# A four-layer graph network on one core: one operand of VectorE's long two-operand instructions moved to PSUM

## The chip, the cores and the metric

The kernel runs on one core of a Trainium2 chip. The metric is the device time in microseconds of one execution, as the median of several runs. The profile is of one further execution; it names the engines PE (TensorE matmul), PEld (TensorE weight load), DVE (VectorE), ACT (ScalarE), POOL (GpSimd) and SP (SyncE). [...] SBUF is the main memory on the core.

## The reference

There are 6250 nodes with 128 features and 100000 directed edges (`src`, `dst`). Four graph layers are added to `x` one after the other, each fed with the rectified layer norm of `x`:

```python
edge_index = jnp.stack([src, dst])
h = relu(_layernorm(x)); x = x + L0(h, src, dst, ...)          # attention, 8 heads
h = relu(_layernorm(x)); x = x + L1(h, edge_index, ...)        # degree-weighted sum, batch norm, relu
h = relu(_layernorm(x)); x = x + L2(h, src, dst, ...)          # attention twice (one head), relu between
h = relu(_layernorm(x)); x = x + L3(h, edge_attr_32, edge_attr_4, edge_weight, edge_weight_n2, src, dst, ...)
```

Layers 0 and 2 weigh the rows of a node's neighbours by a softmax over its incoming edges:

```python
e = leaky_relu(scores_u[src] + scores_v[dst])
m = segment_max(e, dst)
ex = exp(e - m[dst])
out = segment_sum(h[src] * (ex / segment_sum(ex, dst)[dst]), dst)
```

Layer 1 sums scaled rows, `segment_sum(xw[src] * norm[:, None], dst)`, and normalizes over all nodes. Layer 3 works on pairs, the edges once more, with a small perceptron's output `w` for every edge:

```python
w = silu(rbf_ij @ rad_W1 + rad_b1) @ rad_W2 + rad_b2 + (silu(d_gamma @ sph_W1 + sph_b1) @ sph_W2 + sph_b2)
alpha = (q[idx_i] * w * k[idx_j]).sum(-1) / sqrt(32) * cutoff  # 4 heads of 32
agg = segment_sum(alpha[:, :, None] * v[idx_j], idx_i)         # here summed at src, read at dst
```

All arithmetic is float32 in the reference.

## The kernel before

**Blocks.** The nodes are sorted by their number of incoming edges and dealt to 49 blocks of 128 (`NR`). Block `b` has `CAPS[b]` slots for edges: 44, 25, 24, 23 and so on down, 820 in all (`TC`). One slot of a block is one gather: an indirect DMA that POOL issues (`fetch`, line 1577) and that brings 128 rows, one for each node, from a table in HBM. POOL issues some 4360 gathers, one after the other.

**Stages.** After a survey of the edges (0 to 385 us) and the placing of nodes (to 453 us), the stages follow POOL's gathers: layer 0 (`block0`, 453 to 2042 us), layer 1 (`part1`, to 3448), layer 2's first attention, here 2a (`block2` with name `g2`, to 4795), its second, 2b (`block2` with name `g3`, to 6107), and layer 3 (`fast_pairs`, 6125 to 7507).

**One block.** `block0` gathers rows with their scores, DVE forms the scores less their maximum, ACT takes the exponential (1600), DVE multiplies all rows with it (1603, up to 5632 elements per partition), sums them (1605) and the exponentials (1606); then two products on PE, each through `times_in_hops`: transpose into a PSUM tile `th_p` (1079), copy (1082), product into another `th_p` (1086). `block2` is alike, with one head: exponential 1750, product 1753, sums 1755 and 1756. In 2b a block ends with a product of 384 columns: query, key and value of layer 3. The query goes to `own` (1774), key and value are copied to `pr_kv` (1775), and `pair_rows` gathers the block's perceptron outputs from HBM (`pr_e`, 1792, one POOL instruction), multiplies them with the key (1797), and stores product and value as rows of a table in HBM (1801 and 1802, on SP's queue).

**Layer 3.** `fast_pairs` takes these rows by source node, 18 tiles of 128 for each of 49 blocks, three tiles at a time (a group). Gather `fp_rows` (1818, 14 buffers); compare lane numbers with an iota for a one-hot matrix (1823); transpose it (1828), copy it (1831), multiply with the queries (1835); DVE multiplies rows and queries (1838, which reads the PSUM tile `fp_qe`), sums over each head (1840), scales (1841), multiplies the values by these factors (1843); PE adds them up over the one-hot matrix (1849).

**Work behind the blocks.** `Pace` deals three streams of work into the turns of the blocks: the perceptron (`edge_weights`, 1221 to 1278, in layers 0, 1 and 2a), in layer 0 `source_ranks` (1336 to 1353), in layer 1 `source_places`, from about 2080 to 2750 us, and from 4250 us on `source_rows` (1429 to 1449). `source_places` finds the place of each edge among those of its source block: for each of the 49 blocks a row that is 1 where the edge's block equals `n` (1395, bf16 in SBUF), a running sum over it (1397), and a copy of the sum where the row is 1 (1398). A first loop of the same length (1375) makes the same row in order to count it.

**Order.** The order on PE, DVE and ACT is the order of emission (`manual_schedule`): `in_turns` starts block after block and advances the ones in progress by one step in turn, with the work behind dealt in between. A block's rows have three buffers (`rows_tile`), so POOL may run ahead of DVE by two blocks.

Of the kernel before, what the change touches and what calls it, by code (L numbers as in the profile page):

```python
# [27 lines left out]
N, D, E = 6250, 128, 100000  # L28
# [8 lines left out]
NH, HD = 8, 16  # L37
H3, D3 = 4, 32
# [786 lines left out]
NR = 49  # L825
# [11 lines left out]
TC = COL[NR]  # L837
TB = 18
# [233 lines left out]

def times_in_hops(k, p, ps, h, w, width, got):

    nc = k.nc
    nb = h.shape[1]
    t = ps.tile([128, 512], F32, name="th_p").rearrange("p (b d) -> p b d", b=4)
    for b in range(nb):
        nc.tensor.transpose(t[:, b, :], h[:, b, :], k.ident)
    yield  # L1080
    hT = p.tile([128, nb, 128], F32, name="th_T", bufs=3)
    nc.scalar.copy(hT, t[:, :nb, :])
    yield
    y = ps.tile([128, 512], F32, name="th_p")
    for b in range(nb):
        nc.tensor.matmul(y[:, b * width:(b + 1) * width], lhsT=hT[:, b, :], rhs=w, start=True, stop=True)
    got.append(y[:, 0:nb * width].rearrange("p (b f) -> p b f", f=width))
    yield
# [268 lines left out]

def source_places(k, c, q, y):


    nc, tc = k.nc, k.tc
# [3 lines left out]
    b = q.tile([128, TC], I32, name="sp_b")  # L1365
# [24 lines left out]
    pos = k.tile3  # L1390
    nc.vector.memset(pos, -1.0)
    yield
    for n in range(NR):
        eq = q.tile([128, TC], BF16, name="sp_eq", bufs=2)
        nc.vector.tensor_scalar(eq, d, float(n), None, op0=ALU.is_equal)
# [69 lines left out]
def finish(line):  # L1465
    while step(line):
        pass
# [47 lines left out]
def fast_layers(k, x, src, edges, l0, l1, l2a, l2b, l3):  # L1515
# [4 lines left out]
    with ExitStack() as ctx:  # L1520
# [60 lines left out]
        with tc.tile_pool(name="g0s", bufs=1) as q, tc.tile_pool(name="g0s_ps", bufs=2, space=PSUM) as qs, \  # L1581
                tc.tile_pool(name="g0", bufs=2) as p, tc.tile_pool(name="g0_ps", bufs=2, space=PSUM) as ps:
            bigs = big.enter_context(tc.tile_pool(name="g0b", bufs=1, side="right"))

            def block0(b):
# [13 lines left out]
                yield  # L1599
                nc.scalar.activation(e, e, AF.Exp)  # L1600
                yield
# [39 lines left out]
        with tc.tile_pool(name="g1s", bufs=1) as q, tc.tile_pool(name="g1s_ps", bufs=1, space=PSUM) as qs, \  # L1641
                tc.tile_pool(name="g1", bufs=2) as p:
            both = qs.tile([128, 512], F32, name="g1_both")
            total = both[:, 0:2 * D].rearrange("p (a d) -> p a d", a=2)
            spots = source_places(k, later, q, both[:, 2 * D:2 * D + 2 * NR].rearrange("p (a d) -> p a d", a=2))
            parts = [(b, c0, min(WE, CAPS[b] - c0)) for b in range(NR) for c0 in range(0, CAPS[b], WE)]
# [40 lines left out]
            in_turns([part1(*a) for a in parts], turns1, behind)  # L1687
            finish(spots)
            for n in range(2):
                nc.tensor.matmul(total[:, n, :], lhsT=k.ones, rhs=sums[:, n, :], start=True, stop=True)  # L1690
# [43 lines left out]
        for name, table, bias in (("g2", t2, b2), ("g3", t3, b3)):  # L1734
            with tc.tile_pool(name=name, bufs=2) as p, tc.tile_pool(name=name + "_big", bufs=1) as bigs, \
                    tc.tile_pool(name=name + "_ps", bufs=3, space=PSUM) as ps:

                def block2(b, name, table, bias, p, bigs, ps):
                    n = CAPS[b] + 1
# [38 lines left out]
                in_turns([block2(b, name, table, bias, p, bigs, ps) for b in range(NR)], turns_of, behind2)  # L1778
        finish(back.ids)


def pair_rows(k, p, kv, b):

    nc = k.nc
    for c0 in range(0, CAPS[b], WE):
        m = min(WE, CAPS[b] - c0)
        at = k.start_i[:, b:b + 1]
        if c0:
            at = p.tile([128, 1], I32, name="pr_at", bufs=1)
            nc.vector.tensor_scalar(at, k.start_i[:, b:b + 1], c0, None, op0=ALU.add)  # L1790
        e = p.tile([128, WE, D + 2], F32, name="pr_e")
        nc.gpsimd.indirect_dma_start(
            out=e[:, 0:m, :].rearrange("p w d -> p (w d)"), out_offset=None, in_=k.edges,
            in_offset=bass.IndirectOffsetOnAxis(ap=at, axis=0))
        yield
        nc.scalar.copy(e[:, 0:m, D + 1], k.lane[:, COL[b] + c0:COL[b] + c0 + m])
        nc.vector.tensor_tensor(e[:, 0:m, 0:D], e[:, 0:m, 0:D], kv[:, 0:1, :].to_broadcast([128, m, D]), op=ALU.mult)
# [4 lines left out]
        nc.sync.dma_start(to[:, :, D + 2:2 * D + 2], kv[:, 1:2, :].to_broadcast([128, m, D]))  # L1802


def fast_pairs(k, out):
# [3 lines left out]
    TG = 3  # L1809
    with tc.manual_schedule(engines={ET.PE, ET.DVE, ET.Activation}), \  # L1810
            tc.tile_pool(name="fp", bufs=3) as p, tc.tile_pool(name="fp_ps", bufs=2, space=PSUM) as ps:
        held = {}

        def tiles(h, t0):
            rows = p.tile([128, TG, 2 * D + 2], F32, name="fp_rows", bufs=14)
            for t in range(TG):
# [5 lines left out]
            oh = p.tile([128, TG, 128], F32, name="fp_oh", bufs=7)  # L1822
            nc.vector.tensor_tensor(oh, k.iota_l[:, None, :].to_broadcast([128, TG, 128]),
                                    rows[:, :, D + 1:D + 2].to_broadcast([128, TG, 128]), op=ALU.is_equal)
# [13 lines left out]
            nc.vector.tensor_tensor(pr, rows[:, :, 0:D], qe, op=ALU.mult)  # L1838
            al = p.tile([128, TG, H3], F32, name="fp_al")
            nc.vector.tensor_reduce(al, pr.rearrange("p t (h d) -> p t h d", h=H3), axis=AX.X, op=ALU.add)  # L1840
# [117 lines left out]
```

## Time and profile before

| what | us |
|---|---|
| median of 3 runs (7494.39 to 7505.08) | 7500.06 |
| the profiled execution, its own time | 7512.74 |
| its span, first to last instruction | 7510.9 |
| POOL busy | 4424.7 |
| DVE busy | 4015.5 |
| PE busy / PEld busy | 2838.1 / 1890.9 |
| ACT busy | 1178.3 |
| mean granted TensorE clock | 0.648 |

No engine is busy all the time: POOL has 59% of the span, DVE 53%. The span in 40 slices of 188 us shows that the shares change from stage to stage (each digit is a busy share in tenths):

```profile
PE   2301333333423434443344334332323115555555
DVE  9616656565423852233333577656778534545555
POOL 0075555445565775554465676657777756666665
DMA  0232232222221222223122222267878863333333
```

POOL's row is highest in slices 25 to 31, which is 2a's end and 2b; there the DMA row is high too. In a line of a group, the number after `x` is the count of instructions; then come busy us, the mean of one in ns, and the idle time of the engine just before them with what ended most of it. "issue" is time in which the engine waited for nothing that the profile shows, and "remote" is a semaphore whose sender's instruction had ended long before. The chain of waits that ended last covers only the last few microseconds here and says nothing of the rest.

### The profile page before, as it was taken

Reading aid. Unit: us, or ns where it says so; the run is one execution under the profiler, and the core shown is the slowest. Engines: PE = TensorE matmul, PEld = TensorE weight load, DVE = VectorE, ACT = ScalarE, POOL = GpSimd, SP = SyncE. Lnnn points to the kernel's source line nnn. Section 1 sums busy time; section 2 is a strip of 40 time slices with the busy share of each in tenths; the row PEclk is TensorE's granted clock in tenths of the full one; section 3 lists DMA queues with packets and bytes.
Section 4 is the critical chain, followed back from the end, with each engine's and each line's share of the span. In section 5 each row is a group of like instructions: output and inputs, shape, how many; then the busy total and the mean of one; then the engine's idle time right before and its main releaser. Section 6 shows DMA issues by size and latency. Waiting matters only on the chain. (4 is left out here: it accounts for less than half of the span.)

```text
span 7510.9 us, 45920 instructions
## 1 busy us (share of the span) xinstructions
PE 2838.1 (38%) x13095; PEld 1890.9 (25%) x13096; DVE 4015.5 (53%) x7548; ACT 1178.3 (16%) x2275; POOL 4424.7 (59%) x4403
## 2 busy tenths in 40 slices
PE   2301333333423434443344334332323115555555
PEld 2201222222312322222222111100111014544545
DVE  9616656565423852233333577656778534545555
ACT  0201222222301101112122100011122210101111
POOL 0075555445565775554465676657777756666665
PEclk9555656666656766665666566656666557777777
DMA  0232232222221222223122222267878863333333
GB/s 5 63 51 69 73 74 73 71 73 69 65 57 56 72 68 60 65 67 59 51 66 63 51 49 46 42 133 167 180 177 181 179 154 88 89 89 88 89 89 75
DMA packets 456942, 626.12 MB, mean 83 GB/s; under 512 B 83152, under 2 KB 357875, under 8 KB 446836
## 3 DMA queue, kind: packets, MB, share of 16 engines
q0 software_dynamic: 159296, 397.56, 21.5%
q1 hardware_dynamic: 297009, 224.87, 13.1%
q8 instruction: 110, 1.80, 0.1%
q14 instruction: 163, 1.33, 0.1%
q10 hardware_dynamic: 364, 0.57, 0.0%
HBM read 441.86 MB, written 180.80 MB: 83 GB/s over the span
## 5 line engine op out<-in xcount | busy, mean ns | idle before, releaser
L1577 POOL DMA_INDIRECT g_x<-l_t,ell x776 | 761.9, 982 | 683.5 <-DVE g_a L1605 302.8
L1577 POOL DMA_INDIRECT g_x<-l_t,ranks x820 | 805.1, 982 | 542.6 <-DVE g_s L1656 270.7
L1818 POOL DMA_INDIRECT fp_rows<-pair_rows,ids x882 | 861.7, 977 | 440.9 <-issue 195.3
L1577 POOL DMA_INDIRECT g_x<-l2a_t,ranks x776 | 801.4, 1033 | 454.6 <-issue 446.9
L1577 POOL DMA_INDIRECT g_x<-l2b_t,ranks x776 | 867.3, 1118 | 254.2 <-issue 228.9
L1262 PE MATMUL ew_y<-ew_r,ew_g 128*125 128x128 f32 x1600 | 466.0, 387 | 1243.7 <-ACT ew_g L1278 811.6
L1441 PE MATMUL sr_acc<-sr_t,sr_l 128*128 128x441 f16 x1640 | 531.5, 464 | 1056.4 <-DVE sr_l L1449 838.2
L1236 DVE TENSOR_TENSOR ew_out<-ew_y,b 125x512 f32<-125x512 f32 x200 | 137.6, 688 | 1378.4 <-remote 992.4
L1262 PEld LDWEIGHTS ew_y<-ew_r,ew_g 128*125 128x125 f32 x1600 | 368.3, 283 | 1310.4 <-ACT ew_g L1278 898.6
L1849 PE MATMUL fp_acc<-fp_rows,fp_oh 128*128 128x128 f32 x1764 | 352.3, 352 | 617.0 <-issue 217.0
L1447 DVE TENSOR_SCALAR sr_t<-sr_it,sp_tile 128x882 f16<-128x882 f16 x820 | 383.6, 468 | 233.7 <-remote 170.4
L1441 PEld LDWEIGHTS <-sr_l 128*128 128x128 f16 x1640 | 152.3, 114 | 1411.9 <-DVE sr_l L1449 1005.9
L1838 DVE TENSOR_TENSOR fp_pr<-fp_rows,fp_qe 128x384 f32<-128x384 f32 x294 | 162.2, 552 | 596.2 <-remote 409.2
L1849 PEld LDWEIGHTS fp_acc<-fp_rows,fp_oh 128*128 128x128 f32 x1764 | 299.0, 251 | 670.3 <-issue 227.4
L1263 PE MATMUL ew_y<-ew_s,ew_g 128*125 128x128 f32 x1600 | 456.1, 381 | 5.5
L1755 DVE TENSOR_REDUCE g_a<-g_x 128x128 f32<-128x2048 f32 (+13 forms) x96 | 388.9, 4051 | 3.3
L1263 PEld LDWEIGHTS ew_y<-ew_s,ew_g 128*125 128x125 f32 x1600 | 370.0, 284 | 22.4 <-ACT ew_g L1278 12.9
L1278 ACT ACTIVATE ew_g<-ew_h,ew_b 128x500 f32<-128x500 f32 x200 | 135.1, 675 | 1336.2 <-remote 962.7
L1831 ACT COPY fp_ot<-fp_tr 128x384 f32<-128x384 f32 x294 | 137.6, 479 | 1244.9 <-remote 577.5
L1835 PE MATMUL fp_qe<-own,fp_ot 128*128 128x128 f32 x1764 | 324.5, 335 | 12.3 <-issue 10.4
L1835 PEld LDWEIGHTS fp_qe<-own,fp_ot 128*128 128x128 f32 x1764 | 296.7, 248 | 15.7 <-issue 13.0
L1449 DVE TENSOR_SCALAR sr_l<-sr_it,sp_lane,sr_w 128x128 f16<-128x128 f16 x820 | 293.8, 358 | 0.0
(310 smaller groups left out, 6164.2 us busy)
## 6 DMA issues: line engine op xcount, KB each, us to landing
edge_rows<-ew_out SPq DMA_DIRECT2D x50, 910.0 KB
rk_row<-src_lanes SPq DMA_DIRECT2D x164, 160.0 KB
fp_rows<-pair_rows,ids POOLq DMA_INDIRECT x882
g_x<-l_t,ranks POOLq DMA_INDIRECT x820
g_x<-l_t,ell POOLq DMA_INDIRECT x776
g_x<-l2a_t,ranks POOLq DMA_INDIRECT x776
g_x<-l2b_t,ranks POOLq DMA_INDIRECT x776
ew_a<-in_edge_attr_dram SPq DMA_DIRECT2D x25, 448.0 KB
```

Of the source, the lines that this page charges most:

```text
L1236: nc.vector.tensor_tensor(o, y[:EP].rearrange("p (u d) -> p u d", u=4), bias[:EP, None, :].to_broadcast([EP, 4, D]), op=ALU.add)
L1262: nc.tensor.matmul(y[:EP, u * D:(u + 1) * D], lhsT=g[:, 0, e], rhs=m.r2, start=True, stop=False)
L1263: nc.tensor.matmul(y[:EP, u * D:(u + 1) * D], lhsT=g[:, 1, e], rhs=m.s2, start=False, stop=True)
L1441: nc.tensor.matmul(acc[:, h, 0:HT], lhsT=l, rhs=t[:, h * HT:(h + 1) * HT], start=(cc % KG == 0), stop=end)
L1447: nc.vector.tensor_scalar(t, it, k.tile3[:, cc:cc + 1], None, op0=ALU.is_equal)
L1449: nc.vector.tensor_scalar(l, it[:, 0:128], k.lane3[:, cc:cc + 1], weight[:, cc % KG:cc % KG + 1], op0=ALU.is_equal, op1=ALU.mult)
L1577: nc.gpsimd.indirect_dma_start(out=rows[:, j, :], out_offset=None, in_=table, in_offset=bass.IndirectOffsetOnAxis(ap=ids[:, at:at + 1], ax ...
L1755: nc.vector.tensor_reduce(a, v.rearrange("p w d -> p d w"), axis=AX.X, op=ALU.add)
L1818: nc.gpsimd.indirect_dma_start(out=rows[:, t, :], out_offset=None, in_=k.pairs, in_offset=bass.IndirectOffsetOnAxis(ap=k.ids[:, at:at + 1] ...
L1835: nc.tensor.matmul(qe[:, t, :], lhsT=ot[:, t, :], rhs=k.own[:, h, 0:D], start=True, stop=True)
L1838: nc.vector.tensor_tensor(pr, rows[:, :, 0:D], qe, op=ALU.mult)
L1849: nc.tensor.matmul(acc, lhsT=oh[:, t, :], rhs=rows[:, t, D + 2:2 * D + 2], start=(t0 + t == 0), stop=(t0 + t == TB - 1))
```

## The change

One operand of several long instructions of DVE is put in PSUM. In layer 0 and in both halves of layer 2, ACT writes the exponentials to a PSUM tile (`weighed`: two halves by the block's parity in layer 0, four quarters in layer 2), from which the product with the rows and the sum read them. In layer 0 both matrix products of a block use one half each of a second tile (`room`) in place of rotating tiles, since the pool now has one bank less for them. In layer 1 the equality row of the second loop of `source_places` is a float32 row in PSUM (820 of 1024 columns, one buffer) instead of bf16 in SBUF (two buffers). In 2b the key is read by the product of `pair_rows` where the matmul left it, in PSUM; only the value is copied by ACT. In layer 3 the iota of the lanes is copied to PSUM once, and the factors of a group are summed into one of four slots in the same bank, scaled there, and read from there. The instructions stay the same in number and in order, but for that one copy.

```diff
-def times_in_hops(k, p, ps, h, w, width, got):
+def times_in_hops(k, p, ps, h, w, width, got, room=None):
...
-    t = ps.tile([128, 512], F32, name="th_p").rearrange("p (b d) -> p b d", b=4)
+    t = room if room is not None else ps.tile([128, 512], F32, name="th_p")
+    t = t.rearrange("p (b d) -> p b d", d=128)
...
-    y = ps.tile([128, 512], F32, name="th_p")
+    y = room[:, 128:256] if room is not None else ps.tile([128, 512], F32, name="th_p")
...
-        eq = q.tile([128, TC], BF16, name="sp_eq", bufs=2)
+        eq = ps.tile([128, 1024], F32, name="sp_eq")[:, 0:TC]
         nc.vector.tensor_scalar(eq, d, float(n), None, op0=ALU.is_equal)
         run = q.tile([128, TC], F32, name="sp_run", bufs=2)
         nc.vector.tensor_tensor_scan(run, eq, zero, base[:, n:n + 1], op0=ALU.add, op1=ALU.add)
-        nc.vector.copy_predicated(pos, eq.bitcast(U16), run)
+        nc.vector.copy_predicated(pos, eq.bitcast(I32), run)
...
+            weighed = ps.tile([128, 512], F32, name="g0_w")
+            room = ps.tile([128, 512], F32, name="g0_th")
...
-                nc.scalar.activation(e, e, AF.Exp)
+                ex = weighed[:, b % 2 * 256:b % 2 * 256 + n * NH].rearrange("p (w h) -> p w h", h=NH)
+                nc.scalar.activation(ex, e, AF.Exp)
+                e = ex
...
-                yield from times_in_hops(k, p, ps, a, wf, D, y)
+                yield from times_in_hops(k, p, ps, a, wf, D, y, room[:, 0:256])
...
-                yield from times_in_hops(k, p, ps, h[0], w1, D, y)
+                yield from times_in_hops(k, p, ps, h[0], w1, D, y, room[:, 256:512])
...
+                    tc.tile_pool(name=name + "_wps", bufs=1, space=PSUM) as wps:
+                weighed = wps.tile([128, 4, 128], F32, name=name + "_w")
...
-                    nc.scalar.activation(e, e, AF.Exp, bias=s[:, 0:1])
+                    ex = weighed[:, b % 4, 0:n]
+                    nc.scalar.activation(ex, e, AF.Exp, bias=s[:, 0:1])
+                    e = ex
...
-                    kv = p.tile([128, 2, D], F32, name="pr_kv", bufs=3)
+                    kv = p.tile([128, D], F32, name="pr_v", bufs=3)
                     nc.scalar.copy(own[:, b, 0:D], y[0][:, 0, 0:D])
-                    nc.scalar.copy(kv, y[0][:, 0, D:3 * D].rearrange("p (a d) -> p a d", a=2))
-                    yield from pair_rows(k, p, kv, b)
+                    nc.scalar.copy(kv, y[0][:, 0, 2 * D:3 * D])
+                    yield from pair_rows(k, p, y[0][:, :, D:2 * D], kv, b)
...
-        nc.vector.tensor_tensor(e[:, 0:m, 0:D], e[:, 0:m, 0:D], kv[:, 0:1, :].to_broadcast([128, m, D]), op=ALU.mult)
+        nc.vector.tensor_tensor(e[:, 0:m, 0:D], e[:, 0:m, 0:D], key.to_broadcast([128, m, D]), op=ALU.mult)
...
+        both = ps1.tile([128, 512], F32, name="fp_both")
+        lanes = both[:, 0:128]
+        nc.vector.tensor_copy(lanes, k.iota_l)
...
-            nc.vector.tensor_tensor(oh, k.iota_l[:, None, :].to_broadcast([128, TG, 128]),
+            nc.vector.tensor_tensor(oh, lanes[:, None, :].to_broadcast([128, TG, 128]),
                                     rows[:, :, D + 1:D + 2].to_broadcast([128, TG, 128]), op=ALU.is_equal)
...
-            al = p.tile([128, TG, H3], F32, name="fp_al")
+            i = (h * TB + t0) // TG % 4
+            al = both[:, 128 + i * 16:128 + i * 16 + TG * H3].rearrange("p (t h) -> p t h", h=H3)
```

More of the change, by code (lines that the diff above doesn't have):

```diff
@@ L1355, in source_ranks, with source_places @@
         yield
-def source_places(k, c, q, y):
+def source_places(k, c, q, ps, y):
     nc, tc = k.nc, k.tc
@@ L1581, in fast_layers @@
         with tc.tile_pool(name="g0s", bufs=1) as q, tc.tile_pool(name="g0s_ps", bufs=2, space=PSUM) as qs, \
-                tc.tile_pool(name="g0", bufs=2) as p, tc.tile_pool(name="g0_ps", bufs=2, space=PSUM) as ps:
+                tc.tile_pool(name="g0", bufs=2) as p, tc.tile_pool(name="g0_ps", bufs=1, space=PSUM) as ps:
             bigs = big.enter_context(tc.tile_pool(name="g0b", bufs=1, side="right"))
+            weighed = ps.tile([128, 512], F32, name="g0_w")
+            room = ps.tile([128, 512], F32, name="g0_th")
             def block0(b):
@@ L1644, in fast_layers @@
             total = both[:, 0:2 * D].rearrange("p (a d) -> p a d", a=2)
-            spots = source_places(k, later, q, both[:, 2 * D:2 * D + 2 * NR].rearrange("p (a d) -> p a d", a=2))
+            where = ExitStack()
+            spots = source_places(k, later, q, where.enter_context(tc.tile_pool(name="sp_ps", bufs=1, space=PSUM)), both[:, 2 * D:2 * D + 2 * NR].rearrange("p (a d) -> p a d", a=2))
             parts = [(b, c0, min(WE, CAPS[b] - c0)) for b in range(NR) for c0 in range(0, CAPS[b], WE)]
@@ L1688, in fast_layers @@
             finish(spots)
+            where.close()
             for n in range(2):
@@ L1735, in fast_layers, with block2 @@
             with tc.tile_pool(name=name, bufs=2) as p, tc.tile_pool(name=name + "_big", bufs=1) as bigs, \
-                    tc.tile_pool(name=name + "_ps", bufs=3, space=PSUM) as ps:
-                def block2(b, name, table, bias, p, bigs, ps):
+                    tc.tile_pool(name=name + "_ps", bufs=3, space=PSUM) as ps, \
+                    tc.tile_pool(name=name + "_wps", bufs=1, space=PSUM) as wps:
+                weighed = wps.tile([128, 4, 128], F32, name=name + "_w")
+                def block2(b, name, table, bias, p, bigs, ps, weighed):
                     n = CAPS[b] + 1
@@ L1772, in block2, with pair_rows @@
                     yield from times_in_hops(k, p, ps, h[0], w4.rearrange("p a d -> p (a d)"), 3 * D, y)
-                    kv = p.tile([128, 2, D], F32, name="pr_kv", bufs=3)
+                    kv = p.tile([128, D], F32, name="pr_v", bufs=3)
                     nc.scalar.copy(own[:, b, 0:D], y[0][:, 0, 0:D])
-                    nc.scalar.copy(kv, y[0][:, 0, D:3 * D].rearrange("p (a d) -> p a d", a=2))
-                    yield from pair_rows(k, p, kv, b)
-                in_turns([block2(b, name, table, bias, p, bigs, ps) for b in range(NR)], turns_of, behind2)
+                    nc.scalar.copy(kv, y[0][:, 0, 2 * D:3 * D])
+                    yield from pair_rows(k, p, y[0][:, :, D:2 * D], kv, b)
+                in_turns([block2(b, name, table, bias, p, bigs, ps, weighed) for b in range(NR)], turns_of, behind2)
         finish(back.ids)
-def pair_rows(k, p, kv, b):
+def pair_rows(k, p, key, value, b):
     nc = k.nc
@@ L1801, in pair_rows @@
         nc.sync.dma_start(to[:, :, 0:D + 2], e[:, 0:m, :])
-        nc.sync.dma_start(to[:, :, D + 2:2 * D + 2], kv[:, 1:2, :].to_broadcast([128, m, D]))
+        nc.sync.dma_start(to[:, :, D + 2:2 * D + 2], value[:, None, :].to_broadcast([128, m, D]))
 def fast_pairs(k, out):
@@ L1810, in fast_pairs @@
     with tc.manual_schedule(engines={ET.PE, ET.DVE, ET.Activation}), \
-            tc.tile_pool(name="fp", bufs=3) as p, tc.tile_pool(name="fp_ps", bufs=2, space=PSUM) as ps:
+            tc.tile_pool(name="fp", bufs=3) as p, tc.tile_pool(name="fp_ps", bufs=2, space=PSUM) as ps, \
+            tc.tile_pool(name="fp1_ps", bufs=1, space=PSUM) as ps1:
         held = {}
+        both = ps1.tile([128, 512], F32, name="fp_both")
+        lanes = both[:, 0:128]
+        nc.vector.tensor_copy(lanes, k.iota_l)
         def tiles(h, t0):
```

## The prediction

> **What bounds the kernel now.** I read five views in this order: the totals and 40 slices of the page, the groups by line, the same groups with shapes kept apart, the timeline of a stretch of layer 2's second half, and a table of busy times by stage. POOL is the busiest engine (4424.7 us of 7510.9), nearly all of it indirect gathers of 128 rows. The groups show that one gather's mean depends on the stage:
>
> ```profile
> L1577 POOL DMA_INDIRECT g_x<-l_t,ell x776 | 761.9, 982 | 683.5 <-DVE g_a L1605 302.8
> L1577 POOL DMA_INDIRECT g_x<-l_t,ranks x820 | 805.1, 982 | 542.6 <-DVE g_s L1656 270.7
> L1818 POOL DMA_INDIRECT fp_rows<-pair_rows,ids x882 | 861.7, 977 | 440.9 <-issue 195.3
> L1577 POOL DMA_INDIRECT g_x<-l2a_t,ranks x776 | 801.4, 1033 | 454.6 <-issue 446.9
> L1577 POOL DMA_INDIRECT g_x<-l2b_t,ranks x776 | 867.3, 1118 | 254.2 <-issue 228.9
> ```
>
> The row counts instructions, then busy us and mean ns, then idle us before them. With 0.305 us of issue behind each, 776 gathers must be idle 237 us; l2b has 254, so there POOL hardly waits. The other four are idle 170 to 450 us more: they wait for buffers. Why is l2b's gather 1118 ns? The timeline (start, length, engine):
>
> ```profile
> 5497.74 0.94 POOL L1577 DMA_INDIRECT g_x<-l2b_t,ranks  x1 [0.30 <-issue]
> ...
> 5498.68 2.56 DVE L1797 TENSOR_TENSOR pr_e<-pr_e,pr_kv 128x2304 f32<-128x2304 f32 x1 [4.97 <-issue]
> ...
> 5498.99 3.08 POOL L1577 DMA_INDIRECT g_x<-l2b_t,ranks  x1 [0.30 <-issue]
> ...
> 5501.16 2.55 DVE L1753 TENSOR_TENSOR g_x<-g_x,g_e 128x2304 f32<-128x2304 f32 x1
> ...
> 5502.37 2.16 POOL L1577 DMA_INDIRECT g_x<-l2b_t,ranks  x1 [0.30 <-issue]
> 5503.75 4.22 DVE L1755 TENSOR_REDUCE g_a<-g_x 128x128 f32<-128x2304 f32 x1
> 5504.83 0.94 POOL L1577 DMA_INDIRECT g_x<-l2b_t,ranks  x1 [0.30 <-issue]
> ```
>
> A gather takes 0.94 us; one that starts under L1797 ends at 5502.07, 0.83 us after L1797 did (5501.24), and one under L1753 ends at 5504.53, 0.82 us after L1753 (5503.71). L1755, with one operand, holds nothing up. I gave every gather's excess over 0.944 us to the DVE instruction whose end lies 0.82 us (0.75 for the scan L1397) before its own. In us: layer 0 30 (L1603 27); layer 1 31 (L1397 27); 2a 69 (L1753 64); 2b to 5000 us 10, and from there 125 (L1797 68, L1753 51, untouched lines 6); layer 3 34 (L1843 20, L1823 8). About 271 belong to lines that the change touches.
>
> Does an operand in PSUM end this? L1838 is the same kind of instruction, with one operand in PSUM already:
>
> ```profile
> L1838 DVE TENSOR_TENSOR fp_pr<-fp_rows,fp_qe 128x384 f32<-128x384 f32 x294 | 162.2, 552 | 596.2 <-remote 409.2 <-PE fp_tr L1828 76.6 <-issue 48.4
> L1823 DVE TENSOR_TENSOR fp_oh<-iota_l,fp_rows 128x384 f32<-128x384 f32 x294 | 161.9, 551 | 27.7 <-DMA fp_rows<-pair_rows,ids 27.7
> ...
> L1375 DVE TENSOR_SCALAR_CACHE_REDUCE sp_eq<-sp_d 128x820 bf16<-128x820 bf16 x49 | 47.9, 998 | 0.0
> ...
> L1577 POOL DMA_INDIRECT g_x_big<-l2b_t,ranks x44 | 42.0, 955 | 41.1 <-issue 41.1
> ...
> L1395 DVE TENSOR_SCALAR sp_eq<-sp_d 128x820 bf16<-128x820 bf16 x49 | 20.5, 418 | 0.0
> ```
>
> Gathers that overlap L1838 exceed 0.944 by a median of 0 to 2 ns, and it costs what L1823 costs. So I take the mechanism as sound; where POOL's time is path is the question. By stage (length; busy PE, PEld, DVE, ACT, POOL; PE clock, DMA share, GB/s):
>
> ```profile
> 2500.00:2600.00 100.00, 59.65 (x228) 37.11 (x227) 98.09 (x96) 16.50 (x34) 76.85 (x68) 0.74 0.25 73
> 5000.00:5100.00 100.00, 41.98 (x120) 12.71 (x118) 88.41 (x163) 18.36 (x38) 77.52 (x63) 0.67 0.96 212
> 5000.00:6107.00 1107.00, 311.41 (x950) 108.87 (x948) 786.45 (x1489) 239.79 (x492) 832.51 (x747) 0.61 0.81 181
> ```
>
> **The change, part by part.** All sums stand against the profiled execution, 7512.7 us; the median of the runs shown is 12.7 lower, so I subtract 12.7 at the end.
>
> *Keys and exponentials in 2b (L1797, L1753).* From 5000 us POOL has 747 gathers, and its waits beyond issue are some 45 us, 24 of them at the very end. Removed: 68 + 51 = 119 us. Two things take some back. The DMA queues are 0.96 full in the first 100 us, which cannot shrink: 119 × 100/1107 = 11. After that the same bytes pass in less time (0.81 × 1107/988 = 0.91), and the 19.5 us that POOL now waits there for earlier gathers to land I double: 20. Net −88; ends −119 and 0 (POOL's time merely turns into waits, as in the other stages). The 9 us before 5000 sit ahead of a 34 us wait: nothing. ACT copies 128 instead of 256 elements (L1775, 377 ns, towards L1774's 261): 0.1 us a block, covered by ACT's 240 of 1107 busy. L1797 now holds its product's PSUM tile from the matmul until pr_e has landed: around 5460 that is 15 us (matmul 5460.4, L1797 ends 5476.0), of a 26.7 us block that needs two of three tiles. Without that slack the next transposition waits for L1797.
>
> *Exponentials in 2a.* From 4250 us the excess of 37 us lies in runs of 36 to 133 gathers, each ended by a wait of 5 to 28 us (86 together), which a faster POOL only reaches sooner. Before 4250 it is 28 us ahead of waits of 9 to 60. I take a third of 37: −12; ends −64 and 0.
>
> *Layer 0 (L1600, L1603, L1606, and `room`).* 29 waits of 6 to 33 us (447 us) for 30 us of excess: −2; ends −27 and 0. Two products now share one tile's halves; a block's products are read within its 24 × 1.249 = 30 us of gathers, so they do not meet. If that cover went, a transposition would wait for one read (L1615, 0.29 us).
>
> *Layer 1 (L1395, L1397, L1398).* 37 of the 49 equality rows lie in 2500 to 2700 us, where DVE is 98% and then 87% busy. L1395 in bf16 takes 418 ns; float32 into PSUM I price by L1375, 998 ns for the same row at one element per cycle: +0.58 × 37 = +21 us of DVE there. Scan (1938) and copy (1076) stay. Against it POOL loses 25.6 us of blocks between waits ending 2502.7 and 2765.8, and the wait is on DVE (L1656). DVE sets the pace but was not full throughout: +8; ends −15 and +28 (0.58 × 49). With one buffer for the row the next L1395 waits for nothing new, as all three run on DVE in order.
>
> *Layer 3 (L1823, L1840, L1841, L1843).* POOL waits some 2.5 us in 13 gathers for the buffer 14 groups back, so consumers set the pace; 27 us removed is mostly waited again: −4; ends −27 and 0. The extra copy of the lanes is one of 0.3 us.
>
> *Small things.* ACT writing PSUM (L1750 and L1600, 310 ns × 147) and reductions reading it (L1756, 160 ns): between L1774's 261 and L1742's 290 ns for one copy lie 30 ns; ±5 us, off the path.
>
> Sum: −88 − 12 − 2 + 8 − 4 = −98; 7512.7 − 98 − 12.7 = 7402.
>
> [...]
>
> **The rivals.**
>
> *A, slower: relief lost.* DVE and ACT idle long on "remote" (409 us before L1838), which I read as PE's signals arriving late. In the timeline these late signals often come through when POOL has paused or been blocked: 52 of 70 such bursts fall in a pause, 5 under a block. Removing the blocks could lengthen the stalls until POOL runs out of buffers in 2b as in late 2a: 86 us of waits per 336 gathers is 0.256 each, × 747 = 191, less 119: +72; with layer 1's +8 and −10 elsewhere, 7570. It decides from 0.16 us of wait per gather (119/747). For it: layer 1, without blocks, waits about 12 us in 30 gathers. Against: 13 bursts come with POOL at work, and layer 1's waits end with DVE's reduction.
>
> *B, absorbed.* 2b runs into landing waits or DVE (786 of 988 us, 80%), or the operand in PSUM does not free POOL under these wide instructions: the POOL terms vanish, layer 1 costs +8 to +28: 7490 to 7530, say 7505. Against: L1838, and a gather's own wait is small in 2b.
>
> *C, all of it.* 2b −119, late 2a −37: 7512.7 − 156 − 12.7 = 7344; with every block of all stages (271) 7229, which the waits of layers 0, 1 and 3 speak against.
>
> **How the numbers follow.** The forecast has 0.42, C 0.17, B 0.13, A 0.28. About 15 us (0.2%) either way cannot be told from no change. Faster: 0.42 + 0.17 + a little of B = 0.61; same 0.11; slower 0.28. The range runs from just below C, 7320, to 7555, which leaves the worst part of A out; the forecast's own is 7360 to 7450.
>
> **What would show it.** Right: L1577 on l2b falls from 1118 to about 955 ns, l2a from 1033 likewise; 5000 to the start of layer 3 shrinks from 1107 to about 1020; L1395 near 1 us; stages 0, 1 and 3 keep their lengths with longer POOL waits. Wrong: gathers still ending 0.82 us after L1753 or L1797 (mechanism); gathers at 950 ns but 2b as long, with new waits for buffers behind "remote" (A) or for gathers to land (B).

## The result and the profile after

The changed kernel takes 7555.84 us (median of 4 runs) where the kernel before took 7497.79 beside it (also of 4): a ratio of 1.0081, 95% interval 1.0062 to 1.0100. It is slower by 0.8%, and the forecast of faster was wrong. The profile after has a span of 7549.8 us against 7510.9.

The first view is the groups by line of the changed kernel, the five rows of gathers (busy us and mean ns, then idle us before them and what ended most of it):

```profile
L1578 POOL DMA_INDIRECT g_x<-l_t,ranks x820 | 777.0, 948 | 622.3 <-DVE g_s L1663 337.5
L1578 POOL DMA_INDIRECT g_x<-l_t,ell x776 | 737.8, 951 | 685.0 <-DVE g_s L1612 459.8
L1834 POOL DMA_INDIRECT fp_rows<-pair_rows,ids x882 | 837.1, 949 | 461.3 <-issue 193.0
L1578 POOL DMA_INDIRECT g_x<-l2a_t,ranks x776 | 740.6, 954 | 529.5 <-issue 526.5
...
L1578 POOL DMA_INDIRECT g_x<-l2b_t,ranks x776 | 740.3, 954 | 359.7 <-issue 227.4
```

The hold-ups are gone: every stage's gather takes 948 to 954 ns, where layer 2 had 1033 and 1118, and POOL's busy time fell by 267 us (4424.7 to 4157.7). But POOL is idle that much longer, and more. The same groups with shapes kept apart, for two lines that the change touches:

```profile
L1839 DVE TENSOR_TENSOR fp_oh<-fp_both,fp_rows 128x384 f32<-128x384 f32 x294 | 161.8, 550 | 26.0 <-DMA fp_rows<-pair_rows,ids 26.0
...
L1396 DVE TENSOR_SCALAR sp_eq<-sp_d 128x820 f32<-128x820 bf16 x49 | 49.4, 1009 | 0.4
```

Reading an operand from PSUM, which the matmuls write, costs this instruction nothing (550 ns, 551 before), and the float32 row costs what was foreseen (1009 ns, priced at 998). Where the prediction says one element per cycle, the runs show only nanoseconds: 1.04 for each further column of layer 2's product (L1765: 1485 ns at 1280 columns, 2547 at 2304).

Where, then, did the time go? By stages, from a stage's first gather to the next one's, in us:

| | layer 0 | layer 1 | 2a | 2b | layer 3 |
|---|---|---|---|---|---|
| before | 1588 | 1406 | 1347 | 1329 | 1386 |
| changed | 1580 | 1447 | 1369 | 1326 | 1373 |
| difference | −8 | +41 | +22 | −3 | −13 |
| hold-ups of gathers | −25 | −29 | −61 | −126 | |
| POOL's waits beyond issue | +1 | +66 | +81 | +120 | |

The last two rows are the changes in two sums over the gathers of a stage: what each takes over 0.944 us, and what POOL idles over 0.305 us before it, whatever the view puts that down to. The waits gave back the hold-ups in 2b, and more than them in layers 1 and 2a. In layer 1 the loss arises in the stretch of the equality rows: counted from the program's start, the changed kernel is 18 us ahead at this layer's 240th gather or so (7 of them from layer 0), and 44 us behind at the 440th. DVE does not fill that stretch. Here are the rows of busy times, the kernel before first, then the changed kernel:

```profile
2500.00:2770.00 270.00, 120.31 (x449) 78.34 (x447) 204.63 (x198) 34.15 (x70) 196.88 (x182) 0.68 0.23 69
```

```profile
2500.00:2800.00 300.00, 106.71 (x385) 71.46 (x385) 202.68 (x173) 29.95 (x58) 159.61 (x169) 0.62 0.21 55
```

DVE, the third engine of the row, is busy 76% of the time before and 68% after, though its rows are slower. The timeline of the changed kernel shows what it waits for (start, length, engine):

```profile
2506.12 0.63 PE L1264 MATMUL ew_y<-ew_s,ew_g 128*125 128x128 f32 x2
...
2508.35 1.26 PE L1269 MATMUL ew_h<-ew_dT,ew_s 16*128 16x500 f32 x2
...
2514.97 1.08 DVE L1399 COPY_PREDICATED sp_tile<-sp_eq,sp_run 128x820 f32<-128x820 int32 x1
...
2534.77 0.95 POOL L1578 DMA_INDIRECT g_x<-l_t,ranks  x1 [0.30 <-issue]
2539.68 0.69 DVE L1237 TENSOR_TENSOR ew_out<-ew_y,b 125x512 f32<-125x512 f32 x1 [23.64 <-remote]
...
2541.88 0.68 ACT L1279 ACTIVATE ew_g<-ew_h,ew_b 128x500 f32<-128x500 f32 x1 [29.49 <-remote]
...
2557.81 0.94 POOL L1578 DMA_INDIRECT g_x<-l_t,ranks  x1 [22.09 <-DVE g_s L1663]
```

DVE waits 23.6 us for a product of PE (1264) whose last matmul ended at 2506.8, and ACT 29.5 us for one that ended at 2509.6. All the while POOL issues gathers back to back. When it has run out of buffers (2535.7), both signals arrive some 4 to 6 us later. POOL then waits 22 us for DVE, which is late by as much. It is so all through layer 1: POOL pauses 22 times for over 5 us there, and in 20 of these pauses signals that were held arrive, the first at most 6.7 us after POOL's last gather. In the kernel before, the scan held up more than one gather in three of this stretch, and some 125 gathers in a row passed without one late signal.

PE tells the other engines of a finished matmul by incrementing a semaphore: in the changed kernel's trace 3780 matmuls carry an increment, and 3221 increments are there as events. I call a stretch in which these increments arrive over 1 us after their matmul's end a late phase. Late phases are counted from these events; since some are missing, the sums are rough. Layer 1 has 23 (712 us) before and 28 (807 us) after. In the view of the waits they appear as "remote" (us in total, times, longest), here of the changed kernel:

```profile
DVE ew_out L1237 <- remote: 1043.5, 54, 64.7
ACT ew_g L1279 <- remote: 1018.2, 52, 54.8
```

Before, these two stood at 992.4 and 962.7 us. In 2b POOL's gain met another limit. The stage's row of busy times from the first block's end to the last gather, and its group of gathers by what they waited for, in the kernel before:

```profile
4992.00:6079.00 1087.00, 307.34 (x946) 107.69 (x946) 775.04 (x1468) 233.53 (x477) 836.20 (x750) 0.61 0.81 181
...
L1577 POOL DMA_INDIRECT g_x<-l2b_t,ranks x700 | 788.6, 1127 | 231.1 <-issue 205.7 <-DMA g_x<-l2b_t,ranks 19.5 <-DMA pr_e<-edge_rows,start_i 3.3
```

In the changed kernel:

```profile
5047.00:6127.00 1080.00, 329.32 (x946) 110.44 (x946) 770.09 (x1459) 227.47 (x472) 715.56 (x749) 0.60 0.93 182
...
L1578 POOL DMA_INDIRECT g_x<-l2b_t,ranks x704 | 672.0, 955 | 337.1 <-issue 205.3 <-DMA g_x<-l2b_t,ranks 78.1 <-DVE g_s L1768 26.1
```

POOL is busy 716 us where it had 836, but the DMA share rose from 0.81 to 0.93 at the same rate (181 and 182 GB/s), and POOL now waits 78 us for earlier gathers to land, where it had waited 19.5.

### The profile page after: what moved, and what is told of

The parts are those of the page before. It is cut to its first block, busy times and chain, and to the rows that moved or that the text cites. A ratio compares the mean times of both kernels' runs of the same rounds, so it can differ in the third digit from the quotient of the medians.

```text
span 7549.8 us, 45921 instructions
## 1 busy us (share of the span) xinstructions
PE 2917.2 (39%) x13096; PEld 1947.5 (26%) x13096; DVE 4038.0 (53%) x7549; ACT 1174.3 (16%) x2275; POOL 4157.7 (55%) x4403
## 5 line engine op out<-in xcount | busy, mean ns | idle before, releaser
L1578 POOL DMA_INDIRECT g_x<-l_t,ranks x820 | 777.0, 948 | 622.3 <-DVE g_s L1663 337.5
L1578 POOL DMA_INDIRECT g_x<-l_t,ell x776 | 737.8, 951 | 685.0 <-DVE g_s L1612 459.8
L1834 POOL DMA_INDIRECT fp_rows<-pair_rows,ids x882 | 837.1, 949 | 461.3 <-issue 193.0
L1578 POOL DMA_INDIRECT g_x<-l2a_t,ranks x776 | 740.6, 954 | 529.5 <-issue 526.5
L1442 PE MATMUL sr_acc<-sr_t,sr_l 128*128 128x441 f16 x1640 | 556.0, 479 | 1047.6 <-DVE sr_l L1450 594.9
L1578 POOL DMA_INDIRECT g_x<-l2b_t,ranks x776 | 740.3, 954 | 359.7 <-issue 227.4
L1866 PE MATMUL fp_acc<-fp_rows,fp_oh 128*128 128x128 f32 x1764 | 371.6, 366 | 525.9 <-DVE fp_both L1858 264.3
L1866 PEld LDWEIGHTS fp_acc<-fp_rows,fp_oh 128*128 128x128 f32 x1764 | 316.6, 264 | 579.2 <-DVE fp_both L1858 284.9
L1851 PE MATMUL fp_qe<-own,fp_ot 128*128 128x128 f32 x1764 | 345.6, 350 | 42.9 <-issue 25.9
L1851 PEld LDWEIGHTS fp_qe<-own,fp_ot 128*128 128x128 f32 x1764 | 312.9, 261 | 54.0 <-issue 31.7
```

The lines of the kernel that those rows point to most:

```text
L1442: nc.tensor.matmul(acc[:, h, 0:HT], lhsT=l, rhs=t[:, h * HT:(h + 1) * HT], start=(cc % KG == 0), stop=end)
L1578: nc.gpsimd.indirect_dma_start(out=rows[:, j, :], out_offset=None, in_=table, in_offset=bass.IndirectOffsetOnAxis(ap=ids[:, at:at + 1], ax ...
L1834: nc.gpsimd.indirect_dma_start(out=rows[:, t, :], out_offset=None, in_=k.pairs, in_offset=bass.IndirectOffsetOnAxis(ap=k.ids[:, at:at + 1] ...
L1851: nc.tensor.matmul(qe[:, t, :], lhsT=ot[:, t, :], rhs=k.own[:, h, 0:D], start=True, stop=True)
L1866: nc.tensor.matmul(acc, lhsT=oh[:, t, :], rhs=rows[:, t, D + 2:2 * D + 2], start=(t0 + t == 0), stop=(t0 + t == TB - 1))
```

## The experiments

The kernels of one set ran on one chip beside the kernel before. The kernel before itself takes 7447 to 7605 us in some sets and 6468 or 6494 in others, with the same instructions. In the slower sets PE's signals come late as above (over 200 late phases in each kernel without rests), in the quicker ones a trace has at most one late phase. Two sets on a chip of the same number were of both kinds. Stage lengths, in us, and ratios to the kernel before of the same set ("one run": no ratio; e4 and e5 also zero the value columns ahead of layer 0, some 340 us, so only their stages compare):

| set, signals | kernel | layer 0 | layer 1 | 2a | 2b | layer 3 | ratio, interval |
|---|---|---|---|---|---|---|---|
| 1, in time | e1 | 1125 | 1143 | 1045 | 1211 | 1184 | 0.953 (0.952–0.955) |
| | e2 | 1124 | 1152 | 1045 | 1212 | 1184 | 0.955 (0.953–0.957) |
| | e3 | 1124 | 1437 | 1046 | 1213 | 1184 | 0.999 (0.998–1.000) |
| | e4 | 1125 | 1107 | 1046 | 1142 | 1184 | one run |
| 2, late | e7, before | 1602 | 1417 | 1355 | 1389 | 1389 | one run |
| | e6, changed | 1595 | 1496 | 1397 | 1371 | 1388 | 1.009 (1.006–1.012) |
| | e8 | 1605 | 1414 | 1346 | 1332 | 1389 | 0.991 (0.988–0.993) |
| | e5 | 1605 | 1390 | 1337 | 1305 | 1387 | one run |
| 3, in time | e9 | 1127 | 1144 | 1129 | 1246 | 1184 | 0.967 (0.965–0.968) |
| | e10 | 1124 | 1143 | 1046 | 1245 | 1185 | 0.954 (0.952–0.955) |
| | e11 | 1125 | 1437 | 1046 | 1247 | 1183 | 0.999 (0.998–1.000) |
| 4, late | e12, changed | 1582 | 1448 | 1368 | 1297 | 1373 | 1.012 (1.006–1.018) |
| | e13 | 1579 | 1440 | 1376 | 1336 | 1372 | 1.012 (1.006–1.017) |
| | e14 | 1584 | 1392 | 1363 | 1325 | 1374 | 1.003 (1.001–1.006) |
| 5, late | e15 | 1358 | 1312 | 1383 | 1331 | 1372 | 0.967 (0.962–0.973) |
| | e16 | 1311 | 1374 | 1194 | 1349 | 1460 | 0.954 (0.950–0.958) |
| 6, late | e17 | 1276 | 1302 | 1209 | 1365 | 1377 | 0.937 (0.933–0.941) |
| | e18 | 1341 | 1279 | 1199 | 1349 | 1373 | 0.938 (0.934–0.942) |

**Set 1.** e1 takes layer 1's row back (only the row's line is shown; the copy's mask and the PSUM pool go back with it):

```diff
-        eq = ps.tile([128, 1024], F32, name="sp_eq")[:, 0:TC]
+        eq = q.tile([128, TC], BF16, name="sp_eq", bufs=2)
```

> The changed kernel with layer 1's equality row as before (bf16 in SBUF, so the scan and the copy hold POOL's gathers up again). Two theories of layer 1's growth from 1406 to 1447 us. Rests: the signals of PE reach DVE and ACT late while POOL issues gathers without a break, and the scan's hold-ups of the gathers were such breaks. Price: the row takes 1.0 instead of 0.42 us on DVE. Both expect layer 1 back at 1400 to 1412 us and the whole some 35 to 45 us under the changed kernel, 7510 to 7520; if it stays at 1447, neither row nor scan has to do with it.

In the kernel before, layer 1's hold-ups end behind the scan (47 gathers, 27 us) and behind the row itself (15 gathers, 2.6 us); none ends behind the copy.

e2 has the row in float32, but in SBUF, in a tile that it shares with the first loop's row (only the second loop's line is shown):

```diff
-        eq = ps.tile([128, 1024], F32, name="sp_eq")[:, 0:TC]
+        eq = q.tile([128, TC], F32, name="sp_eq")
```

> The changed kernel with layer 1's equality row in float32 in SBUF: if the row stays slow (1.0 us), the price is kept while the scan reads two operands from SBUF again and holds the gathers up. Price: layer 1 stays at 1430 to 1450 us. Rests: 1400 to 1420 us, with the gathers held up again (mean well over 948 ns) and no waits of 20 us in the stretch of the equality rows. If the row runs faster than 0.7 us here, the run says little on the price.

e3 gives POOL rests among layer 1's gathers, in the changed kernel:

```diff
+                gone[0] += 1
+                if gone[0] % 6 == 0 and any(table is t for t in (t1,)):
+                    for _ in range(7):
+                        nc.gpsimd.memset(rest, 0.0)
```

> The changed kernel with a rest for POOL in layer 1: after every sixth gather seven small fills of a scratch tile, some 2 us together, 136 times. Rests: in spite of some 270 us more of POOL's work, the long idle times on remote signals (24 of over 5 us, 694 us in all) shrink to less than half, and layer 1 takes 1340 to 1440 us. Price (or any theory in which PE's late signals have nothing to do with the gathers): POOL's fills come on top in part, 1447 to 1700 us, and the late signals stay as they are.

e4 drops 2b's second store, of 820 × 128 rows of 512 bytes (54 MB, a quarter of the stage's 200; the 100 MB of the expectation are all its stores):

```diff
-        nc.sync.dma_start(to[:, :, D + 2:2 * D + 2], value[:, None, :].to_broadcast([128, m, D]))
```

> The changed kernel without the store of the value rows in layer 2b (the table's value columns are zeroed once, before layer 0, so layer 3's sum is left out of the output): 100 MB less of 200 MB of stores and gathers, about a quarter of the bytes that the stage moves. Transfers: 2b is limited by its DMA traffic (share 0.93), so from the first block's end to the last gather it takes 980 to 1020 us instead of 1080. Stalls: PE's late signals limit it, 1050 us or more.

This set had PE's signals in time, so the first three could not tell the two theories apart, but they showed something else. The kernel before took 6468 us, e1 4.7% less. The group of the instruction that had waited 1043 us on remote signals, in e10, which is e1's kernel, by its waits:

```profile
DVE ew_out L1237 <- PE ew_y L1264: 166.7, 49, 5.8
```

With signals in time POOL sets the pace (e1: layer 0 1125 us for 868 × 1.249 = 1084 of gathers), and a hold-up costs nearly its full length (83 of 87 us in 2a, e9 against e10). There the slow row costs nothing that shows: layer 1 takes 1107 us with it in PSUM (e4) and 1143 with the fast row and hold-ups (e1). e2's row took 643 ns, in the range that I had set as telling little on the price; its 1152 us follow the hold-ups, not the row. e3's rests are pure loss, 1437 against 1107. e4's 2b is 69 us shorter than e1's (1142 against 1211): its transfers take that much of the stage even without late signals.

**Set 2.** The changed kernel and the kernel before once more; 2b's part alone (e8, here against the changed kernel; e1's edit is in it too and not shown, and layer 0's `room` and layer 3's copy of the lanes stay); and the kernel before without the value store, by the same edit as e4's (e5).

```diff
-                nc.scalar.activation(ex, e, AF.Exp)
+                nc.scalar.activation(e, e, AF.Exp)
...
-                    ex = weighed[:, b % 4, 0:n]
+                    ex = weighed[:, b % 4, 0:n] if name == "g3" else e
...
-            nc.vector.tensor_tensor(oh, lanes[:, None, :].to_broadcast([128, TG, 128]),
+            nc.vector.tensor_tensor(oh, k.iota_l[:, None, :].to_broadcast([128, TG, 128]),
...
+            al = p.tile([128, TG, H3], F32, name="fp_al")
```

> The changed kernel itself. In the runs e1 to e4 no signal of PE came late (one phase of over 1 us, against 239 in the changed kernel's own profile) and the kernel before took 6468 us there, not 7498. Two theories of that gap: the late signals belong to the chip, or to something that comes and goes. If this chip is one without late signals, POOL sets the pace and the change is worth its hold-ups: layers 0, 1 and 2a take their gathers times 1.25 us (1104, 1027 and 1028 us), and the whole takes 6120 to 6140 us, 0.945 to 0.95 of the kernel before. If the late signals are back, it is slower than the kernel before by 0.5 to 1%.

> The kernel before itself, for its profile on this chip. Without late signals: POOL gathers without waits in layers 0, 1, 2a and 2b, at the same means as in the first profile or longer (982, 982, 1033, 1118 ns), the hold-ups are the path, and the sum of their excess over 944 ns is about the gain of the changed kernel here. With late signals: as the first profile, 7500 us.

> The kernel before with the change in layer 2b alone (exponentials and keys in PSUM). Without late signals: 100 to 135 us less than the kernel before, if transfers let it (the stage's own hold-ups, 136 us); if the DMA traffic limits the stage, 30 to 70. With late signals: within 15 us of the kernel before, since what POOL gains is waited for landings and late signals.

> The kernel before without the store of the value rows in layer 2b (the table's value columns are zeroed once, before layer 0; layer 3's sum is left out of the output). POOL sets layer 2b's pace before the change: the stage takes within 25 us of the kernel before's. If transfers set it already, it is 60 us shorter or more.

Here the signals are late, and the result repeats: 1.0086, with layer 1 +79 us and 2a +42. e8, which has these two stages as before, takes 1414 and 1346 us there, as the kernel before does (1417 and 1355): so 2a's loss goes when 2a's part of the change goes, in which no instruction of DVE grew longer (e14 below, with 2a changed and layer 1's row not, keeps it: 1363). 2b's part alone gains 0.9% and 57 us in its stage (1389 to 1332), more than expected for late signals, less than half of the 119 us of hold-ups that it removes. The value store left out takes 84 us from 2b even in the kernel before (1389 to 1305): its transfers set part of the pace already, against my view of the stage as POOL's alone.

**Set 3.** e9 has layers 1 and 2a as before (e1's edit and the second one of e8's); e10 and e11 are e1 and e3 again.

> The changed kernel with layers 1 and 2a as before (row in SBUF in layer 1, exponentials in SBUF in 2a); layers 0, 2b and 3 stay changed. On a chip with late signals of PE (the kernel before takes 7500 to 7600 us): 0.985 to 0.995 of the kernel before, as in the run with 2b alone (0.991), since the two stages that lost are undone. On a chip without (6468 us): 0.955 to 0.965, some 50 us worse than with 2a changed.

> The changed kernel with layer 1's equality row as before, once more, in case this chip has late signals. If it has: layer 1 from its first gather to 2a's first takes 1400 to 1420 us as in the kernel before (the changed kernel took 1447 and 1496 in its two profiles), and the ratio to the kernel before is 0.995 to 1.003. If it hasn't: 0.953 again.

> The changed kernel with POOL's rests in layer 1 (after every sixth gather seven small fills, 137 times), once more. If the chip has late signals and rests let them through: the late phases of layer 1 fall from 28 (some 810 us) to fewer than half of that time, and layer 1 takes no longer than in the changed kernel (1447 to 1496 us) though POOL has some 330 us more to do. If the late signals don't care for short rests, layer 1 grows by 100 to 330 us and the late phases stay.

The signals were in time again, and the ratios of e10 and e11 repeated set 1's to 0.1%. e9 against e10 gives the price of 2a's hold-ups: 1129 against 1046 us. With signals in time the parts add: e10 is 296 us under the kernel before, and layer 1's row would add 36 (1143 to 1107), worked out from e4 and e10; the whole change itself was not run in such a set, and would stand near 0.949.

**Set 4.** The changed kernel (e12), with e3's edit (e13) and with e1's (e14), this time with late signals:

> The changed kernel. Where PE's signals come in time (before: 6470 to 6500 us), its layers 0, 1 and 2a take their gathers times 1.25 us as in the run with rests and in those with layer 1 as before, so 6120 to 6170 us, 0.942 to 0.950 of the kernel before. Where they come late (before: 7500 to 7600 us), 1.005 to 1.012.

> The changed kernel with POOL's rests in layer 1. With late signals, and if rests let them through: layer 1 no longer than in the changed kernel of this call, its late phases less than half. With late signals, and if short rests do nothing: layer 1 100 to 330 us longer than the changed kernel's, the phases as they were. Without late signals: 0.999 of the kernel before, as twice already.

> The changed kernel with layer 1's equality row as before. With late signals: layer 1 some 40 to 70 us shorter than the changed kernel's of this call, so that all of the loss is layer 1's. Without: 30 to 40 us longer (1062 against 1027 us), the ratio 0.953.

The row as before (e14) takes layer 1 from 1448 to 1392 us: the hold-ups are back, and POOL waits less. The gathers of e12, then of e14:

```profile
L1578 POOL DMA_INDIRECT g_x<-l_t,ranks x820 | 776.5, 947 | 625.6 <-DVE g_s L1663 340.1 <-issue 282.5 <-DMA g_x<-l_t,ranks 3.0
```

```profile
L1578 POOL DMA_INDIRECT g_x<-l_t,ranks x820 | 808.5, 986 | 536.4 <-issue 283.6 <-DVE g_s L1662 249.7 <-DMA g_x<-l_t,ranks 2.7
```

e13 tells what these waits come from. Its groups of POOL:

```profile
L1580 POOL DMA_INDIRECT g_x<-l_t,ranks x820 | 778.2, 949 | 273.0 <-issue 273.0
...
L1585 POOL MEMSET rest<- 128x256 bf16 x959 | 303.6, 317 | 47.1
```

The gathers of layer 1 wait for nothing but their issue. The waits within layer 1, e12 (changed) first, then e13:

```profile
ACT ew_g L1279 <- remote: 691.8, 28, 54.7
DVE ew_out L1237 <- remote: 500.1, 25, 64.7
POOL g_x L1578 <- DVE g_s L1663: 340.1, 26, 23.6
```

```profile
DVE ew_out L1237 <- PE ew_y L1264: 79.6, 28, 4.0
```

The remote waits are gone, the late phases fell from 28 (826 us) to one of 2 us, and the stage takes 1440 us instead of 1448, though POOL has 304 us of fills on top. DVE's slow row is in both, and so is the operand in PSUM. So neither of these, nor DVE's load, makes POOL wait by itself; PE's late signals do, and breaks between the gathers let them through. How much of the 56 us between e12 and e14 is the row's price, paid while DVE is behind, was not measured apart, as e2 ran only in time.

**Sets 5 and 6.** How long must a break be? The rests of e3, in more layers, with other numbers:

```diff
+                for t, every, times in ((t0, 6, 3), (t1, 10, 4), (t2, 4, 1)):
+                    if table is t and gone[0] % every == 0:
```

> The changed kernel with shorter or rarer rests of POOL, in three layers: layer 0 three fills after every 6th gather (0.94 us each time, worked out from the fills' 0.364 us in the run with rests), layer 1 four after every 10th (1.3 us), layer 2a one after every 4th (0.2 us). In the run with rests 2.4 us after every 6th gather took layer 1's late phases from 28 (826 us) to one of 2 us. With late signals, where a setting lets them through, its stage takes its gathers times 1.25 us and the rests: layer 0 about 1230 us instead of 1540, layer 1 1130 instead of 1360, 2a 1070 instead of 1340; where it doesn't, the stage stays as it was. Some of the three should do, so 0.90 to 0.97 of the kernel before. Without late signals: 0.945 of the kernel before plus 276 us of rests, 0.985 to 0.99.

e16 has `(t0, 10, 7), (t1, 6, 2), (t2, 6, 3)`, and in layer 3 three fills where `at % 6 == 0`:

> As e15 with other settings: layer 0 seven fills after every 10th gather (2.4 us), layer 1 two after every 6th (0.57 us), layer 2a three after every 6th (0.94 us), layer 3 three after every 6th. With late signals, where a setting does: layer 0 1300 us, layer 1 1105, 2a 1156, layer 3 1300 instead of 1370; where it doesn't, the stage stays. 0.90 to 0.97 of the kernel before. Without late signals: plus 540 us of rests, 1.02 to 1.03.

e17 has `(t0, 12, 7), (t1, 10, 7), (t2, 6, 3)`, e18 `(t0, 10, 5), (t1, 8, 5), (t2, 8, 4)`:

> The changed kernel with the settings that the two before point to: layer 0 seven fills (2.4 us) after every 12th gather, layer 1 seven after every 10th, layer 2a three (0.94 us) after every 6th, none in layer 3, where the rests lost 90 us. With late signals: layer 0 about 1290 us (1311 at every 10th), layer 1 1310 instead of 1374, 2a 1194, the rest as in the changed kernel; in all about 6960 us, 0.925 to 0.94 of the kernel before. Without: plus some 500 us of rests, 1.01 to 1.03.

> As e17 with rests of middle length: layer 0 five fills (1.67 us) after every 10th gather, layer 1 five after every 8th, layer 2a four (1.3 us) after every 8th. If a rest must be over some 2 us to let the signals through in layers 0 and 1, they stay late there and the run is 0.945 to 0.965; if less does, the lower sum of rests makes it 0.92 to 0.94. Without late signals: 1.00 to 1.015.

Late phases left over, in us, by the break's length and how often it comes: layer 0 (690 to 740 without) 470 with 0.94 us after every 6th gather, 520 with 1.67 after every 10th, 91 and 216 with 2.4 after every 10th and 12th. Layer 1 (800 to 830): 795 with 0.57 after every 6th, 744 with 1.3 after every 10th, 14 with 1.67 after every 8th, 33 with 2.4 after every 10th. Layer 2a (630 to 700): 736 with 0.2 after every 4th, 339 and 332 with 0.94 after every 6th, 237 with 1.3 after every 8th. So in layer 1, at every 10th gather, 1.3 us does not let the signals through and 2.4 does; 1.67 does at every 8th. In layer 0 1.67 us at every 10th is too little and 2.4 does, and in 2a 0.94 already helps. But late phases are not the stage's length. In layer 1 of e15 they stayed at 744 us, and the stage took 1312 us all the same, near e17's 1302 with 33: POOL's waits beyond issue fell from 334 us (e12) to 95 and 1. There a late phase cost as far as POOL had to wait for it. Rests in layer 3 lost 88 us (1460 against 1372). e18 was both of its cases at once: layer 0's signals stayed late, layer 1's and 2a's came. e17's groups show what is left of POOL's waits:

```profile
L1580 POOL DMA_INDIRECT g_x<-l_t,ranks x820 | 776.5, 947 | 259.7 <-issue 257.7 <-DMA g_x<-l_t,ranks 1.8 <-DVE sp_base L1382 0.3
L1580 POOL DMA_INDIRECT g_x<-l2b_t,ranks x776 | 741.0, 955 | 412.1 <-issue 235.1 <-DVE g_s L1775 123.2 <-DMA g_x<-l2b_t,ranks 30.7
L1580 POOL DMA_INDIRECT g_x<-l2a_t,ranks x776 | 737.7, 951 | 245.4 <-issue 245.4
L1580 POOL DMA_INDIRECT g_x<-l_t,ell x776 | 737.4, 950 | 229.0 <-issue 224.7 <-DMA g_x<-l_t,ell 1.2 <-DVE g_s L1608 0.6
```

In layers 0, 1 and 2a POOL hardly waits any more (1, 1 and 27 us beyond issue); in 2b and layer 3 it does (176 and 173). e17 takes 6979 us where the kernel before took 7447 beside it: 6.3% less, with the changed kernel at 1.01 in such sets. Where the signals come in time it was not run; there 2.4 us after every 6th gather of layer 1 alone cost 330 us (e3, e11 against e4), so it should lose to the plain changed kernel.

## Why the prediction was wrong

**The mechanism** of the hold-ups was right in each part: gathers fell to 954 ns as said (955 foreseen for 2b), DVE's busy time rose by 22 us (4015.5 to 4038.0), no more than the slow row's price, and the row costs 1.0 us. With signals in time the change gives 4.7% without its row in layer 1.

**The step that failed** is the cost of a removed hold-up in a stage that waits elsewhere. I wrote for 2a that its excess lies ahead of waits "which a faster POOL only reaches sooner", and gave it −12; I gave layer 1 +8, weighing DVE's price (+21) against POOL's gain (25.6). Both took a hold-up's removal to be worth nothing at worst. It was worth less than nothing: the hold-ups were breaks that let PE's signals pass. 2a came out at +22 (+42 in set 2), layer 1 at +41 (+79; +56 from e14 to e12). For layer 1 I had read POOL's wait on DVE as DVE setting the pace, from a row with DVE 98% busy between 2500 and 2600 us; once the hold-ups were gone DVE was busy 61% of these 100 us, and idle 24 us on one late signal. e13 shows that without late signals the slow row makes POOL wait for nothing; for 2a, where DVE had no price to pay, e8 and the rests of e16 to e18 (1194 to 1209 us, 1368 in e12) show it.

**2b**, −88 in the sum, came out at −3 (−18 in set 2, −57 for its part alone). The terms for transfers were mis-sized: I let the landing waits grow by 20 us, from 19.5; they grew by 58, to 78, with the DMA share at 0.93, which I had put at 0.91, and the value store alone accounts for 69 to 84 us of the stage (e4, e5). Late phases grew too, 206 to 265 us (162 to 384 in set 2); how the rest divides between these two was not separated.

**Layers 0 and 3** were small, as forecast: −8 and −13 against −2 and −4.

**Rival A** named the cause, relief lost, and its sign, at 0.28; its place was wrong. It set the loss in 2b, from 0.16 us of wait per gather (it came to 120 us over 870 gathers, 0.14, so just short of it), and gave layer 1 only DVE's price, where the stretch of the scans was the longest one of layers 0 to 2a without a late phase in the kernel before. What I had set against it, 13 late bursts that came with POOL at work, weighed too much beside 52 that came in its pauses. **Rival B**, absorbed, fits 2b, which ran into landing waits, but not layers 1 and 2a. **Rival C**, all of it, is what the sets with signals in time show, and more: there a hold-up costs nearly its full length (2a: 87 us of hold-ups and 83 of time between e9 and e10), since POOL hardly waits.

## What to carry to other kernels

A wait marked "remote", behind a matmul long ended, was a second bottleneck here (1043 us ahead of one line of DVE): before a stall beside such a wait is removed, ask whether the stall is what ends it, by setting the times of release against the other engines' pauses over the whole trace. The test for it is cheap: put idle work where the stall was. With 304 us of it on top, layer 1 got no longer (1440 us in e13, 1448 in e12), so breaks of that kind were worth their cost here. And where the kernel before differs by 14% between sets, a ratio belongs to its set; parts are compared by stage within one.

## What the runs showed of the hardware

- PE's semaphore increments came late while POOL issued indirect gathers back to back (1.25 us each): in the changed kernel's layer 1 there are 28 late phases with 807 us together, and waits of up to 64.7 us on them. In 20 of POOL's 22 pauses there the first held increment arrived at most 6.7 us after its last gather. There are 215 to 240 late phases, of some 3 ms in all, in a run of 7.5 to 7.7 ms, and none to speak of in sets where the same programs take 6.2 to 6.5 ms. What makes a set of the one kind or the other stays open, and so does the path on which the signals are held.
- Breaks of POOL of 1.67 to 2.4 us after every 6th to 10th gather, made of fills of 0.32 us, took nearly all of them away in layer 1 (826 us in e12 to 2, 14 and 33 in e13, e18 and e17).
- A gather held up by DVE ended 0.82 us after the DVE instruction (L1797 and L1753 in the kernel before, 0.81 to 0.82 us in 124 gathers), and 0.75 us after the scan (L1397, 47 gathers).
